# Two-layer graph attention on one core: empty slots of layer 1's gathers get an index past the table's end, and their rows are not read

## The chip, the core and the metric

The kernel runs on one core of a Trainium2 chip. The metric is the device time of one execution in microseconds. Three runs of the kernel before gave 1804.87, 1805.07 and 1805.76 us, so the median is 1805.07 us. One more execution was taken with the hardware profiler, and all durations below come from it.

## The reference

A graph has 3125 nodes with 768 features and 53,125 edges (`src`, `dst`, sorted by `dst`; 25,000 drawn edges in both directions and one self loop for each node). The features are normalised and passed through relu, then two graph attention layers follow, each with a layer norm and a dense residual. The result is added to `x`.

```python
def gat_conv(x, src, dst, W, a_src, a_dst, bias, heads, out_ch, concat):
    xl = (x @ W).reshape(n, heads, out_ch)                 # layer 1: 4 x 256, layer 2: 1 x 768
    alpha_src = jnp.einsum('nhc,hc->nh', xl, a_src)
    alpha_dst = jnp.einsum('nhc,hc->nh', xl, a_dst)
    e = jax.nn.leaky_relu(alpha_src[src] + alpha_dst[dst], 0.2)
    e = jnp.exp(e - jax.ops.segment_max(e, dst, n)[dst])
    alpha = e / (jax.ops.segment_sum(e, dst, n)[dst] + 1e-16)
    return jax.ops.segment_sum(xl[src] * alpha[:, :, None], dst, n) + bias
...
h = relu(layernorm(x))
h1 = relu(layer_norm(gat_conv(h, layer 1))) + (h @ Wr1 + br1)
h2 = layer_norm(gat_conv(h1, layer 2)) + (h1 @ Wr2 + br2)
return x + h2
```

What matters here is the last line of `gat_conv`: for each node, the rows `xl[src]` of its edges are weighted and added.

## The kernel before

**Slots.** The nodes are cut into 25 blocks of 128 (the last has 53). Each block has 17 tiles of 128 slots (the last block has 8), and each slot holds one edge of the block. The four quarters of a block, 32 nodes each, start at slot 0, 512, 1024 and 1536, or where the quarter before has ended if that is later. A node's last self loop takes no slot: its row is added from a plain load (`own`). So the 416 tiles have 53,248 slots, and 50,000 edges fill them. For every slot `rel_s` holds the edge's destination within its block, or -1 where the slot is empty, and `idx_s` holds its source node, or 0 where the slot is empty (L393, L398).

**Stages.** Up to about 300 us the kernel computes `table1` (the rows `xl` of layer 1, 4 KB each, in HBM), packs the slots and looks up the attention terms of destinations. From there to about 500 us it finds the terms of the sources (L1049 to L1060, with the one-hot `ohh` made from `hi_s`, the high part of the source's number) and the softmax weights `al` (`weights`, L576). Then `sums` (L633) does layer 1's sums, and from about 1210 us the second layer runs with a loop of its own.

**Layer 1's sums.** For each tile `fetch` (L685) lets GpSimd issue one indirect DMA (L692), which reads 128 rows of `table1` by the tile's column of `idx_s` into a buffer `g` of 512 KB. There are 13 buffers, taken in turn. `weights_of` (L706) lets VectorE make the tile's matrix `w`: a one-hot of `rel_s` (`oh`, L712) times the softmax weights (L713). An empty slot has `rel_s` = -1, which no column equals, so its weights are 0. TensorE multiplies `w` with `g` into PSUM (`pa`, L732), 256 columns at a time and four quarters beside each other. The tiles of a block come in five rounds (`ROUNDS`): 0, 5, 9, 13; 1, 6, 10, 14; 4, 11, 15; 2, 8, 16; 3, 7, 12. The tiles of the next round are fetched right after a round's matmuls are written down.

**What sets the order.** TensorE, ScalarE and VectorE run in the order in which the program is written. `step` (L644) mixes other work between the rounds: the end of the block before (`end1`, L1123: norm, transposes, and the product with W2, `p` in L182, whose rows go to `table2`), and the residual product of a few late blocks (`more`, `pr` in L182). GpSimd issues the gathers in order. A gather waits until TensorE has read the buffer that it will fill (the gather 13 before), and until the gather 8 before it has landed, since there are eight semaphores in turn (`DMASW0` to `DMASW7`). Once per block GpSimd also gathers the softmax totals (`ao`, L678). The first 13 gathers need no buffer to come free and are issued as soon as `table1` is stored. SyncE's queue carries the plain loads and stores beside the gathers.

The buffers lie in memory that other tiles used before. After the first 13 gathers each buffer holds rows of `table1` in all 128 partitions.

Of the kernel before, what the change touches and what calls it, by code (L numbers as in the profile page):

```python
# [10 lines left out]
F32 = mybir.dt.float32  # L11
# [3 lines left out]
I32 = mybir.dt.int32  # L15
I16 = mybir.dt.int16
AF = mybir.ActivationFunctionType
OP = mybir.AluOpType
# [12 lines left out]
J = 17  # L31
# [4 lines left out]
CODE = 4096  # L36
# [6 lines left out]
@with_exitstack  # L43
def preln_gat2_kernel(
    ctx: ExitStack,
    tc: tile.TileContext,
    x, src, dst,
    W1, a_src1, a_dst1, b1, g1, be1, Wr1, br1,
    W2, a_src2, a_dst2, b2, g2, be2, Wr2, br2,
    out,  # L50
):

    pool = ctx.enter_context(tc.tile_pool(name="flag", bufs=1))
    flag = pool.tile([1, 1], I32, name="flag")
    in_order(tc, x, src, dst, W1, a_src1, a_dst1, b1, g1, be1, Wr1, br1,  # L60
             W2, a_src2, a_dst2, b2, g2, be2, Wr2, br2, out, flag)
    other = tc.nc.values_load(flag[0:1, 0:1], min_val=0, max_val=1)
    with tc.If(other > 0):
        any_order(tc, x, src, dst, W1, a_src1, a_dst1, b1, g1, be1, Wr1, br1,
                  W2, a_src2, a_dst2, b2, g2, be2, Wr2, br2, out)
# [3 lines left out]
def in_order(  # L69
# [16 lines left out]
    nc = tc.nc  # L86
    N, D = x.shape
# [5 lines left out]
    NB = -(-N // P)  # L93
# [28 lines left out]
    def tiles_of(b):  # L122
        return J if b < NB - 1 else JL
# [34 lines left out]
    rel_s = const.tile([128, NB * J], F32, name="rel_s")  # L158
    idx_s = const.tile([128, NB * J], I32, name="idx_s")
    hi_s = const.tile([128, NB * J], F32, name="hi_s")  # L160
    has = const.tile([128, 3, NB], F32, name="has")
    at_last = const.tile([128, NB], I32, name="at_last")
    quarter_i = const.tile([128, 1], I32, name="quarter_i")
# [25 lines left out]
    def load_rows(q, t, src_, b):  # L189

        for o, e in pieces(b):
            q.dma_start(t[o:e], src_[b * P + o:b * P + e, :])
# [440 lines left out]
    def sums(heads, cols, table, al, alo_d, ahead, lag, gp, ap, pp, end, more, pace, first=None, delay=0.0):  # L633
# [4 lines left out]
        width = heads * cols  # L638
        f = width // 2
# [36 lines left out]
        def ask(b):  # L676
            ao = asked[b] = ap.tile([128, 2 * heads, NB], F32, name="ao", bufs=3)
            nc.gpsimd.indirect_dma_start(  # L678
                out=ao.rearrange("p v b -> p (v b)"), out_offset=None, in_=alo_d[:, :],
                in_offset=bass.IndirectOffsetOnAxis(ap=at_last[:, b:b + 1], axis=0))  # L680

        turns = count()
        owns = {}

        def fetch(b, k):  # L685

            got = {}
            for j in ROUNDS[k]:
                if j >= tiles_of(b):
                    continue  # L690
                g = gp.tile([128, width], F32, name=f"g{next(turns) % ahead}", bufs=1)
                nc.gpsimd.indirect_dma_start(  # L692
                    out=g, out_offset=None, in_=table[:, :],
                    in_offset=bass.IndirectOffsetOnAxis(ap=idx_s[:, b * J + j:b * J + j + 1], axis=0))
                got[j] = g, weights_of(b, j)
                place = PLACE[j]
                if place == 4:
                    own = owns[b] = ap.tile([128, width], F32, name="own", bufs=3)
                    load_rows(nc.sync, own, table, b)
                if b == 1 and place == 11:  # L700
                    ask(0)
                if b and place == (13 if tiles_of(b) == J else 5):
                    ask(b)
            return got

        def weights_of(b, j):  # L706

            c = b * J + j
            lo, hi = 32 * QUARTERS[j][0], 32 * QUARTERS[j][-1] + 32
            w = ap.tile([128, heads, hi - lo], F32, name=f"w{hi - lo}", bufs=9 if hi - lo == 32 else 3)  # L710
            oh = ap.tile([128, 68], F32, name="oh", bufs=4)[:, :hi - lo]
            nc.vector.tensor_scalar(oh, iota_f[:, lo:hi], rel_s[:, c:c + 1], None, op0=OP.is_equal)  # L712
            nc.vector.tensor_tensor(w, oh[:, None, :].to_broadcast([128, heads, hi - lo]),  # L713
                                    al[:, POS[j], :, b:b + 1].to_broadcast([128, heads, hi - lo]), OP.mult)
            return w
# [32 lines left out]
    with tc.tile_pool(name="m1", bufs=1) as mp:  # L748
# [8 lines left out]
        with tc.tile_pool(name="h0", bufs=1) as hp, tc.tile_pool(name="pm1", bufs=1, space=PSUM) as pm1, \  # L757
# [238 lines left out]
            with tc.tile_pool(name="pq1", bufs=1, space=PSUM) as pp:  # L996
                with tc.tile_pool(name="sb1", bufs=1) as sb:
# [62 lines left out]
                        next(slots, None)  # L1060
                    for _ in slots:
                        pass
                with tc.tile_pool(name="sr1", bufs=1) as sr:
                    weights(H, own, al1, alo1, keep1, sr, xs1, pp, 4, fill, (5, 13, 8))
                for _ in fill:
# [115 lines left out]
    with tc.tile_pool(name="m2", bufs=1, reuse_waits="tile") as mp, \  # L1181
# [3 lines left out]
        f = C2 // 2  # L1185
# [708 lines left out]
```

## Time and profile before

| | us |
|---|---|
| median of 3 runs | 1805.07 |
| profiled execution | 1801.14 |
| its span, first to last instruction | 1799.2 |
| TensorE busy, whole span | 1637.3 |
| GpSimd busy, whole span | 885.9 |
| first gather of layer 1's sums issued | 307.62 |
| first matmul of layer 1's sums | 503.37 |
| last gather of layer 1 issued | 1153.6 |
| first gather of layer 2 issued | 1211.1 |

The time of an execution is a little more than the span, since it holds what lies before the first and after the last instruction: 1801.14 beside 1799.2 us. In the views, "busy" is the time in which an engine works on instructions, and "idle before" is the time in which it stood still before an instruction, with what ended that wait behind an arrow. PE is TensorE's matmuls, PEld its weight loads, DVE VectorE, ACT ScalarE and POOL GpSimd. `g<-table,idx_s` is a gather; L692 is layer 1's and L1280 layer 2's. The DMA share is the busy share of the 16 DMA engines, and values a little over 1 come from overlapping packets.

### The profile page before, as it was taken

The numbers are of one execution on the slowest core, as the hardware profiler recorded it, in microseconds if no ns is written. First come the engines' busy times: TensorE is split into PE (matmuls) and PEld (weight loads), VectorE is DVE, ScalarE is ACT, GpSimd is POOL, SyncE is SP. The second block draws the span as 40 slices with busy tenths as digits, with TensorE's granted clock in tenths as the row PEclk, the third lists the DMA queues.
The fourth block names the chain that finished last, engine by engine and source line by source line (L and its number), as shares of the span: only waits on it lengthen the run. The fifth ranks groups of instructions, "written<-read, shape, count | busy, mean of one in ns | idle before, by whom it ended". The sixth has DMA issues, their size and how long they took to land. (4 is left out here: it accounts for less than half of the span.)

```text
span 1799.2 us, 43360 instructions
## 1 busy us (share of the span) xinstructions
PE 1637.3 (91%) x17747; PEld 870.2 (48%) x17747; DVE 998.1 (55%) x2639; ACT 454.1 (25%) x1286; POOL 885.9 (49%) x922
## 2 busy tenths in 40 slices
PE   8999999899968999999999999996988888888885
PEld 5666665566534555556554555532333333333331
DVE  7683443788865466566566565632444444444445
ACT  2222332000121222122122112122333333333342
POOL 2000111100055566666566666506777777777772
PEclk9999999999988999999999999998999999999997
DMA  7834546633199999999999999939999999999994
GB/s 239 275 104 136 147 114 192 233 131 123 36 341 407 381 407 407 409 405 410 406 400 411 411 398 400 401 104 387 367 387 380 376 386 386 372 386 384 378 345 148
DMA packets 173719, 562.56 MB, mean 313 GB/s; under 512 B 28610, under 2 KB 53976, under 8 KB 173384
## 3 DMA queue, kind: packets, MB, share of 16 engines
q0 software_dynamic: 100912, 402.06, 58.1%
q1 hardware_dynamic: 68206, 147.26, 23.0%
q10 hardware_dynamic: 4394, 10.39, 1.5%
q8 instruction: 142, 2.33, 0.5%
q14 instruction: 65, 0.53, 0.1%
HBM read 498.62 MB, written 65.62 MB: 314 GB/s over the span
## 5 line engine op out<-in xcount | busy, mean ns | idle before, releaser
L692 POOL DMA_INDIRECT g<-table,idx_s x416 | 407.6, 980 | 404.1 <-DVE m L613 174.7
L1280 POOL DMA_INDIRECT g<-table,idx_s x416 | 421.5, 1013 | 179.2 <-issue 63.7
L732 PE MATMUL pa<-g,w 128*32 128x256 f32 x3912 | 276.5, 389 | 32.0 <-DMA g<-table,idx_s 21.1
L182 PE MATMUL pr<-wr,h 128*32 128x384 f32 (+1 forms) x3136 | 292.4, 504 | 0.0
L182 PE MATMUL p<-w,h1T 128*32 128x384 f32 (+1 forms) x3136 | 283.9, 489 | 2.6 <-DVE h1T L1152 2.6
L732 PEld LDWEIGHTS pa<-g,w 128*32 128x32 f32 x3912 | 144.6, 112 | 146.1 <-issue 28.7
L1347 PE MATMUL pa<-g,w 128*32 128x384 f32 x1956 | 196.3, 509 | 3.1 <-DVE v L1372 3.1
L182 PEld LDWEIGHTS p<-w,h1T 128*32 128x32 f32 x3136 | 123.1, 110 | 125.6 <-issue 85.8
L713 DVE TENSOR_TENSOR w<-oh,al 128x128 f32<-128x128 f32 (+1 forms) x416 | 132.0, 317 | 80.4 <-PE pa L732 45.5
L182 PEld LDWEIGHTS pr<-wr,h 128*32 128x32 f32 (+1 forms) x3136 | 100.6, 112 | 151.0 <-issue 150.1
L1314 DVE CUSTOM_DVE_ANT_0 e<-mix,pen 128x640 f32<-128x640 f32 x25 | 20.6, 824 | 245.5 <-PE mix L1311 245.5
L182 PE MATMUL pr<-h0k,wr 128*32 128x256 f32 (+1 forms) x2304 | 146.9, 391 | 0.9 <-DMA h0k<-h0T_d 0.9
L837 PE MATMUL pm<-w,h0l 128*128 128x344 f32 (+1 forms) x468 | 140.8, 455 | 0.0
L1293 ACT ACTIVATE slots<-g 128x32 f32<-128x32 f32 x416 | 75.1, 222 | 231.4 <-DMA g<-table,idx_s 229.5
L974 PE MATMUL pm<-h0g,wr 128*128 128x512 f32 x288 | 131.7, 604 | 0.0
L837 PE MATMUL pm<-w,h0g 128*128 128x344 f32 x432 | 130.8, 459 | 0.3 <-ACT h0g L816 0.3
L905 POOL DMA_DIRECT2D hot_d<-ohd x25 | 13.4, 537 | 220.1 <-DVE own L491 121.0
L1347 PEld LDWEIGHTS pa<-g,w 128*32 128x32 f32 x1956 | 67.9, 116 | 110.5 <-issue 97.7
L712 DVE TENSOR_SCALAR oh<-iota_f,rel_s 128x32 f32<-128x32 f32 (+1 forms) x416 | 110.9, 267 | 0.1
L182 PEld LDWEIGHTS pr<-h0k,wr 128*32 128x32 f32 x2304 | 80.5, 111 | 55.0 <-issue 9.2
L837 PEld LDWEIGHTS pm<-w,h0l 128*128 128x128 f32 (+1 forms) x468 | 84.8, 185 | 44.1 <-issue 5.7
L1311 PE MATMUL mix<-ident,slots 128*128 128x128 f32 x125 | 22.5, 319 | 88.1 <-ACT slots L1293 88.1
(282 smaller groups left out, 1704.5 us busy)
## 6 DMA issues: line engine op xcount, KB each, us to landing
s<-slo_d SPq DMA_DIRECT2D x25, 544.0 KB
g<-table,idx_s POOLq DMA_INDIRECT x832
table<-row SPq DMA_DIRECT2D x24, 512.0 KB
own<-table SPq DMA_DIRECT2D x24, 512.0 KB
h1T_d<-h1T SPq DMA_DIRECT2D x24, 512.0 KB
h<-h1T_d SPq DMA_DIRECT2D x22, 512.0 KB
table<-row SPq DMA_DIRECT2D x24, 392.0 KB
ring<-in_x_dram SPq DMA_DIRECT2D x24, 384.0 KB
```

The costliest lines, as they stand in the source:

```text
L182: nc.tensor.matmul(out_[o:e], lhsT[:, o:e], rhs, start=start, stop=stop, skip_group_check=True)
L692: nc.gpsimd.indirect_dma_start(out=g, out_offset=None, in_=table[:, :], in_offset=bass.IndirectOffsetOnAxis(ap=idx_s[:, b * J + j:b * J + ...
L712: nc.vector.tensor_scalar(oh, iota_f[:, lo:hi], rel_s[:, c:c + 1], None, op0=OP.is_equal)
L713: nc.vector.tensor_tensor(w, oh[:, None, :].to_broadcast([128, heads, hi - lo]), al[:, POS[j], :, b:b + 1].to_broadcast([128, heads, hi - ...
L732: nc.tensor.matmul(pa[32 * q:32 * q + 32, o // f, o % f:o % f + n], w[:, o // cols, :], g[:, o:o + n], start=to not in opened, stop=False, ...
L837: nc.tensor.matmul(pm[:r, :C], h0[b][:, k, :], w1[:, k, i * C:(i + 1) * C], start=(k == 0), stop=(k == NK1 - 1))
L974: nc.tensor.matmul(pm, wr1[:, k, m * 128:(m + 1) * 128], groups[gi][:, k, :], start=(k == 0), stop=(k == NK1 - 1))
L1280: nc.gpsimd.indirect_dma_start(out=g, out_offset=None, in_=table2[:, :], in_offset=bass.IndirectOffsetOnAxis(ap=idx_s[:, b * J + j:b * J + ...
L1293: nc.scalar.activation(slots[b % 2][:, POS[j], :], gs[b, j][:, C2:C2 + 1].to_broadcast([128, 32]), AF.Copy)
L1311: nc.tensor.transpose(mix[:, c * 128:(c + 1) * 128], at[:, o:o + 4].rearrange("p q n -> p (q n)"), ident)
L1314: nc.vector.tensor_tensor_reduce(out=e, in0=mix[:, :WIN], in1=pen, scale=1.0, scalar=-BIG, op0=OP.add, op1=OP.max, accum_out=top)
L1347: nc.tensor.matmul(pa[32 * q:32 * q + 32, i, :f], w_, g[:, i * f:(i + 1) * f], start=(i, q) not in opened, stop=False, skip_group_check=True)
```

## The change

A second list of indices, `idx_k`, takes the memory of `hi_s`, whose last reader has then run. It equals `idx_s` where a slot holds an edge, and `idx_s + 4096` where it holds none. VectorE makes it in two instructions at the end of the stage of the sources' terms. In layer 1's sums the first 13 gathers go by `idx_s` as before; each later one goes by `idx_k` and carries a bound, `N - 1` = 3124, with `oob_is_err=False`: an index past the bound is no error, and its row is not read. The slot's partition of `g` then keeps what an earlier gather put there, and its weight is 0. In the built program a register move, which writes 3124, stands ahead of each of these gathers on GpSimd. Layer 2 goes by `idx_s` as before.

```diff
     hi_s = const.tile([128, NB * J], F32, name="hi_s")
+    idx_k = hi_s.bitcast(I32)
...
-                g = gp.tile([128, width], F32, name=f"g{next(turns) % ahead}", bufs=1)
-                nc.gpsimd.indirect_dma_start(
-                    out=g, out_offset=None, in_=table[:, :],
-                    in_offset=bass.IndirectOffsetOnAxis(ap=idx_s[:, b * J + j:b * J + j + 1], axis=0))
+                turn = next(turns)
+                g = gp.tile([128, width], F32, name=f"g{turn % ahead}", bufs=1)
+                c = slice(b * J + j, b * J + j + 1)
+                if turn < ahead:
+                    nc.gpsimd.indirect_dma_start(
+                        out=g, out_offset=None, in_=table[:, :],
+                        in_offset=bass.IndirectOffsetOnAxis(ap=idx_s[:, c], axis=0))
+                else:
+                    nc.gpsimd.indirect_dma_start(
+                        out=g, out_offset=None, in_=table[:, :],
+                        in_offset=bass.IndirectOffsetOnAxis(ap=idx_k[:, c], axis=0),
+                        bounds_check=N - 1, oob_is_err=False)
...
                     for _ in slots:
                         pass
+                    none = sb.tile([128, NB * J], F32, name="none")
+                    nc.vector.tensor_scalar(none, rel_s, 0.0, float(CODE), op0=OP.is_lt, op1=OP.mult)
+                    nc.vector.tensor_tensor(idx_k, none, idx_s, OP.add)
```

On VectorE two instructions come in. The rows below are VectorE's order before, at the last two blocks of the sources' terms (`ohh` is the one-hot of a source's high part, `scr<-pq,ohh` the products that pick the term out, `al` the terms themselves).

```order
L545 TENSOR_REDUCE al_116<-scr 128x68 [waits DVE_49]
L1056 TENSOR_TENSOR ohh<-iota_f,hi_s 128x425
L542 TENSOR_TENSOR scr<-pq,ohh 128x500 [waits DVE_49,PE_49]
L542 TENSOR_TENSOR scr<-pq,ohh 128x500 [waits PE_49] x2
L542 TENSOR_TENSOR scr<-pq,ohh 128x200 [waits PE_49]
```

The same place on VectorE with the change:

```order
L546 TENSOR_REDUCE al_116<-scr 128x68 [waits DVE_49]
L1065 TENSOR_TENSOR ohh<-iota_f,hi_s 128x425
L1074 TENSOR_TENSOR hi_s<-none,idx_s 128x425 [waits DVE_49]
L543 TENSOR_TENSOR scr<-pq,ohh 128x500 [waits PE_49] x3
L543 TENSOR_TENSOR scr<-pq,ohh 128x200 [waits PE_49]
```

The add that writes `idx_k` (named `hi_s` here, whose memory it takes) stands between the last `ohh` and the products that use it. The other new instruction, `none<-rel_s`, stands some 170 instructions earlier on VectorE, at the start of the stage. On TensorE, ScalarE and SyncE nothing moves.

On GpSimd the gathers keep their places and their waits. Before, around the fourteenth gather of layer 1:

```order
L692 DMA g_4503<-table_64,idx_s 128x1024 [waits DMASW0_49,DVE_49]
L692 DMA g_4509<-table_64,idx_s 128x1024 [waits DMASW1_49]
L692 DMA g_4515<-table_64,idx_s 128x1024 [waits DMASW2_49,PE_49]
L692 DMA g_4551<-table_64,idx_s 128x1024 [waits DMASW3_49,PE_49]
L692 DMA g_4557<-table_64,idx_s 128x1024 [waits DMASW4_49,PE_49]
```

With the change:

```order
L696 DMA g_4506<-table_64,idx_s 128x1024 [waits DMASW0_49,DVE_49]
L696 DMA g_4512<-table_64,idx_s 128x1024 [waits DMASW1_49]
L700 DMA g_4518<-table_64,hi_s 128x1024 [waits DMASW2_49,PE_49]
L700 DMA g_4556<-table_64,hi_s 128x1024 [waits DMASW3_49,PE_49]
L700 DMA g_4564<-table_64,hi_s 128x1024 [waits DMASW4_49,PE_49]
```

From the fourteenth on the list of indices is the new one; each gather waits for the same lane of semaphores and the same engine as before.

## The prediction

> **What bounds the kernel now.** I read the page's slices first: they say where each engine and the DMA engines are full.
>
> ```profile
> span 1799.2 us, 43360 instructions
> ...
> PE   8999999899968999999999999996988888888885
> ...
> DMA  7834546633199999999999999939999999999994
> GB/s 239 275 104 136 147 114 192 233 131 123 36 341 407 381 407 407 409 405 410 406 400 411 411 398 400 401 104 387 367 387 380 376 386 386 372 386 384 378 345 148
> ```
>
> A slice is 45 us. From the 12th to the 26th, about 500 to 1170 us, stands layer 1's sums. The DMA engines move some 405 GB/s there and TensorE is full too, so either could be the one that sets the pace. The table of windows tells them apart, for the starting stretch, the steady part in two pieces, and the tail:
>
> ```profile
> core 0: us, PE busy (x) PEld busy (x) DVE busy (x) ACT busy (x) POOL busy (x), PEclk, DMA share, GB/s
> 520.00:580.00 60.00, 45.72 (x585) 25.01 (x581) 28.30 (x100) 7.70 (x20) 35.62 (x38) 0.80 1.03 408
> 580.00:800.00 220.00, 219.09 (x3440) 119.19 (x3436) 128.41 (x433) 46.35 (x134) 139.09 (x145) 1.00 1.02 401
> 800.00:1165.00 365.00, 351.28 (x5090) 196.09 (x5085) 225.00 (x747) 71.87 (x204) 236.62 (x249) 1.00 1.02 405
> 1165.00:1215.00 50.00, 46.88 (x466) 19.40 (x460) 17.84 (x56) 10.48 (x26) 3.53 (x5) 0.97 0.38 132
> ```
>
> TensorE stands still for 60 - 45.72 = 14.3 us in the start, 220 - 219.09 = 0.9 us up to 800, 365 - 351.28 = 13.7 us up to 1165, and 3.1 us in the tail: 32.0 us in all. So faster transfers can give no more than 32.0 us, although the DMA engines are full for 650. What ends those waits is in the list of TensorE's waits, asked for 520 to 580 and then for 800 to 1165:
>
> ```profile
> PE pa L732 <- DMA g<-table,idx_s: 12.0, 9, 3.8
> PE pa L732 <- DVE z L670: 2.3, 1, 2.3
> ...
> PE pa L732 <- DMA g<-table,idx_s: 9.2, 12, 1.5
> PE pa L732 <- DVE oh L712: 3.1, 3, 1.9
> PE pa L732 <- DVE aw L666: 1.2, 1, 1.2
> ```
>
> Gathers end 12.0 of the first 14.3 us and 9.2 of the later 13.7. The rest is ended by VectorE, which itself waits for TensorE to free the buffers of `w`, as the groups of 520 to 1215 show:
>
> ```profile
> L713 DVE TENSOR_TENSOR w<-oh,al 128x128 f32<-128x128 f32 x330 | 97.2, 295 | 76.6 <-PE pa L732 45.5 <-DVE oh L712 1.4
> ```
>
> Between 580 and 800 no gather is waited for at all: there TensorE alone sets the pace.
>
> **What is removed.** The slots count 416 x 128 = 53,248, the edges in them 50,000, so 3248 rows are not read. Placing the edges of the inputs by the rules of the windows gives where: none in the first 13 gathers, in 54 of the other 403, mostly in tile 16, a block's fourteenth gather. Block 0 has 123 empty slots, block 1 has 135 (116 in tile 16, 19 in tile 3), block 2 has 74, blocks 3 to 8 have 868, 9 and 10 have 216, and 11 to 24 have 1832. A row is 4096 B, so at 405 GB/s it costs 10.1 ns of all 16 engines, and 3248 rows cost 32.8 us. How much of this is on the path is decided stretch by stretch.
>
> *Start, 520 to 580.* TensorE waits here for one gather after the other, so DMA time is path time. The last wait rows of it:
>
> ```profile
> 553.34 3.89 PE L732 MATMUL pa<-g,w 128*32 128x256 f32 x28 [1.41 <-DMA g<-table,idx_s]
> 558.46 1.03 PE L732 MATMUL pa<-g,w 128*32 128x256 f32 x2 [1.23 <-DMA g<-table,idx_s]
> 560.95 3.20 PE L732 MATMUL pa<-g,w 128*32 128x256 f32 x26 [1.46 <-DMA g<-table,idx_s]
> ```
>
> Counted in the program's order, the matmuls of 561 us are those of block 2's first rounds; its tile 16 comes in the fourth, after the waits. So 123 + 135 = 258 rows count: 258 x 10.1 ns = 2.6 us.
>
> Which of the 16 engines has a row could change this. The Trainium skill, "DMA: Bandwidth & Descriptors", section The descriptor swizzle, says that one engine serves partitions 0 to 3 and 32 to 35, and so on for the others. No view here shows a packet's engine. The empty slots are the last ones of tile 16 (5 to 127 in block 0, 12 to 127 in block 1), so by that rule this engine would be spared 4 + 4 of its rows, not 16; a gather has landed when its last engine is done, and the term would be 1.3 us in place of 2.6.
>
> *580 to 800.* No time on the path. The 868 rows of blocks 3 to 8 and the 216 of 9 and 10 make the DMA engines 10.9 us earlier; what shows is a longer lead of the gathers before TensorE, as far as 13 buffers hold it.
>
> *800 to 1165.* The idle time comes in stretches:
>
> ```profile
> 800.00:850.00 50.00, 49.70 (x768) 31.17 (x763) 32.44 (x109) 10.55 (x30) 33.47 (x36) 1.00 1.03 410
> 850.00:900.00 50.00, 46.40 (x656) 25.53 (x644) 29.20 (x98) 6.72 (x18) 30.06 (x31) 0.97 1.03 406
> 900.00:950.00 50.00, 50.00 (x777) 26.20 (x780) 30.91 (x104) 10.57 (x31) 33.04 (x35) 1.00 1.01 401
> 950.00:1000.00 50.00, 46.57 (x675) 25.55 (x671) 32.39 (x110) 9.02 (x25) 31.98 (x34) 1.00 1.03 411
> 1000.00:1050.00 50.00, 45.57 (x612) 27.42 (x607) 32.51 (x109) 9.19 (x25) 32.16 (x34) 1.00 1.03 411
> 1050.00:1100.00 50.00, 50.00 (x749) 26.42 (x745) 25.87 (x86) 11.75 (x36) 33.14 (x36) 1.00 1.01 399
> 1100.00:1150.00 50.00, 48.03 (x703) 24.71 (x699) 35.09 (x115) 9.90 (x28) 34.75 (x36) 1.00 1.02 394
> ```
>
> The DMA time removed is 1832 x 10.1 ns = 18.5 us in 365, or 2.5 us in each 50. The longest stretch, 950 to 1050, idles 3.4 + 4.4 = 7.9 us; 5.1 us are removed within it and 2.5 in the 50 ahead of it, so it is covered to within 0.3. The others are covered with room. So I take it that the waits for gathers go, 9.2 us, and of the 4.5 us behind VectorE about half, since VectorE's buffers come free earlier when TensorE waits less: 11.4 us, between 9.2 and 13.7. What is late next is TensorE itself.
>
> *The tail.* Layer 2's first gather waits for the last row of `table2`, and the chain that ended last shows it:
>
> ```profile
> 1196.78 10.32 PE p L182 x43
> ...
> 1207.98 0.32 SPq L196
> ...
> 1211.09 7.56 DMA g<-table,idx_s
> ```
>
> TensorE's last products lead to the store and the store to layer 2, so what TensorE gains passes on to layer 2 undiminished. Layer 2 itself keeps its gathers.
>
> **What is added.** *VectorE:* two instructions on 128x425. The nearest rows are the one-hot of the same size and the products behind it, at the end of the sources' stage:
>
> ```profile
> 457.44 0.59 DVE L1056 TENSOR_TENSOR ohh<-iota_f,hi_s 128x425 bf16<-128x425 f32 x1
> 458.48 2.29 DVE L542 TENSOR_TENSOR scr<-pq,ohh 128x500 f32<-128x500 f32 x4 [0.45 <-PE pq L540]
> ...
> 465.12 2.29 DVE L542 TENSOR_TENSOR scr<-pq,ohh 128x500 f32<-128x500 f32 x4 [2.39 <-PE pq L540]
> ```
>
> The add, some 0.6 us, stands just behind that `ohh`. The wait of 0.45 us hides most of it and the next wait for TensorE, 2.39 us, the rest. The compare stands at the start of the stage and is as long; every wait in between takes it up. I count nothing; without that cover it would be 1.2 us. The fourteenth gather now also needs `idx_k`, which is 50 us old by then.
>
> *GpSimd:* nothing in the trace shows a gather with a bound. Its price decides the sign, so here are the rows around it: layer 1's gathers from 520 to 1215, the total's gathers, two gathers issued back to back, and a plain DMA issue of GpSimd.
>
> ```profile
> L692 POOL DMA_INDIRECT g<-table,idx_s x397 | 381.9, 962 | 215.2 <-issue 86.7 <-DMA g<-table,idx_s 58.1 <-PE pa L732 52.9
> L678 POOL DMA_INDIRECT ao<-alo_d,at_last x25 | 25.0, 998 | 13.3 <-DMA g<-table,idx_s 4.8 <-DVE oh L712 4.5 <-issue 3.2
> ...
> 316.17 0.94 POOL L692 DMA_INDIRECT g<-table,idx_s  x1 [0.30 <-issue]
> 317.42 0.94 POOL L692 DMA_INDIRECT g<-table,idx_s  x1 [0.30 <-issue]
> ...
> L905 POOL DMA_DIRECT2D hot_d<-ohd x25 | 13.4, 537 | 220.1 <-DVE own L491 121.0 <-DVE ohd L508 73.0 <-DVE own_r L492 22.9
> ```
>
> A gather takes 0.94 us and 0.30 us pass to the next even with nothing to wait for. Of the idle 215.2 + 13.3 us, 422 x 0.30 = 126.6 are this, so 102 us are true waiting: 102 / 397 = 0.26 us a gather is free. Below that, a dearer gather hides behind buffers and landings. The price of the bound lies between below nothing (fewer rows to write descriptors for, in 54 gathers; these issues are off the path anyway) and, as an upper row, what handling 128 indices costs now: 0.94 - 0.54 = 0.40 us. I take under 0.1 us, the register move and a compare, since the indices are already walked one by one; that is hidden.
>
> **Sum.** Against the profiled 1801.1 us: -2.6 - 11.4 = -14.0, so 1787.1. Against the median, 3.9 us higher: 1805.1 - 14.0 = 1791.1 us. A difference under 0.2%, 3.6 us, can hardly be told from none.
>
> **The rivals.**
>
> *GpSimd becomes the bound, slower.* At 0.40 us more, 397 x 0.40 = 159 us meet 102 free: +57 us, 1862, and the saving in rows is worth nothing, since the transfers then wait for their issue. It decides from 0.26 us a gather. For it speaks how little room there is; against it that the instruction and its list of 128 indices are the same. The Trainium skill, "GPSIMD Engine Reference", section 3.1, speaks for it: branching that depends on data costs about 12 cycles an element; at its 1.2 GHz an estimate from that page is 128 x 10 ns = 1.28 us a gather on one core, and the kernel would take some 2200 us. No row shows such a branch. Chance 0.24.
>
> *TensorE is the bound anyway.* If the waits after 800 only change their releaser from gathers to VectorE's `oh` and `w`, the start's 2.6 us is all: 1802.5, within 0.2%. For it: 4.5 us already end at VectorE. Against it: VectorE is busy for 225 of 365 us. Chance 0.08.
>
> *The rows are not spared.* If an index past the bound still takes a transfer of its slot, everything stays: 1805.1. The trace has no such gather. Chance 0.08.
>
> **How the numbers follow.** The forecast has 0.60. Its low end: the weight loads wait for gathers as well, and if that time lay wholly beside the matmuls' waits, it would add to the gain.
>
> ```profile
> PEld pa L732 <- DMA g<-table,idx_s: 10.6, 9, 1.9
> ```
>
> That is 2.6 + 13.7 + 10.6 = 26.9 us, 1778; I take 1779. The high end must take in both cases without gain (1802.5, 1805.1) and the mild part of the first rival, 0.02 us a gather past the threshold: 397 x 0.02 = 8 us, 1813. Beyond it lies most of the first rival, some 0.2. Faster by over 0.2%: 0.60; within: 0.16; slower: 0.24.
>
> **What would show it.** Right: back-to-back gathers of layer 1 still some 1.24 us apart; the software queue's bytes lower by 3248 x 4096 B = 13.3 MB; TensorE's waits for `g` after 800 near 0 and idle time from 800 to 1165 under 5 us; in the start 2 to 3 us less; layer 2's first gather 14 us earlier and layer 2 as long as before. The forecast is wrong if gathers of layer 1 are 1.5 us or more apart with nothing to wait for (first rival), if TensorE idles as long with VectorE as releaser (second), or if the bytes stay (third).

## The result, and the profile after

The changed kernel takes 1790.45 us, the median of 6 runs (1787.15 to 1801.98), against 1804.62 us for 6 runs of the kernel before beside it (1797.27 to 1805.76). The ratio is 0.9933, with a 95% interval of 0.9909 to 0.9956: 12 us less, 8 to 16 with the interval. The two medians lie 14.2 us apart and the two profiled spans 11.4. The profiled execution took 1789.67 us, its span 1787.8. The forecast was 1791.1, which is 14.0 us less than the 1805.1 it set out from.

First, were rows spared? The row of the software queue says so, here of the kernel before and then, with the page's slices, of the one after:

```profile
q0 software_dynamic: 100912, 402.06, 58.1%
```

```profile
DMA  7833545633179999999999999929999999999994
GB/s 239 270 103 131 150 122 170 258 124 129 42 288 406 362 384 401 391 402 391 407 398 396 410 380 363 391 87 393 362 382 382 380 387 386 377 384 383 371 348 159
...
q0 software_dynamic: 100912, 388.76, 57.3%
```

13.30 MB are gone, which is 3248 rows of 4096 B. The number of packets is unchanged at 100,912: in place of each spared row a small packet is left, and the page's count of packets under 512 B rises by 3248, from 28,610 to 31,858. The slices still show full DMA engines through layer 1's sums, at a slightly lower rate.

Where the time went can be seen if the span is cut at the same work in both kernels: from the first matmul of layer 1's sums (`pa`) in four pieces to the first gather of layer 2. The windows before:

```profile
core 0: us, PE busy (x) PEld busy (x) DVE busy (x) ACT busy (x) POOL busy (x), PEclk, DMA share, GB/s
503.40:595.80 92.40, 74.70 (x969) 43.73 (x973) 44.85 (x145) 14.22 (x34) 54.68 (x53) 0.83 1.02 404
595.80:802.10 206.30, 205.39 (x3206) 109.83 (x3202) 125.35 (x424) 44.47 (x128) 132.09 (x138) 1.00 1.02 401
802.10:1174.30 372.20, 358.48 (x5164) 199.19 (x5158) 230.70 (x763) 72.16 (x205) 235.67 (x248) 1.00 1.02 404
1174.30:1211.10 36.80, 33.68 (x313) 13.34 (x309) 10.13 (x31) 8.62 (x24) 0.01 (x1) 0.95 0.17 54
```

And after:

```profile
505.20:595.40 90.20, 74.13 (x968) 43.46 (x972) 45.73 (x145) 14.23 (x34) 57.21 (x53) 0.87 1.02 400
595.40:801.10 205.70, 205.42 (x3207) 108.84 (x3202) 127.00 (x424) 44.47 (x128) 139.92 (x139) 1.00 1.00 386
801.10:1165.50 364.40, 354.06 (x5164) 193.48 (x5158) 230.66 (x763) 72.17 (x205) 246.41 (x246) 1.00 1.00 389
1165.50:1200.60 35.10, 31.98 (x313) 12.72 (x309) 10.13 (x31) 8.53 (x23) 0.01 (x1) 1.00 0.17 56
```

The matmul counts agree to one, so each pair is the same work:

| stretch | before | after | difference |
|---|---|---|---|
| up to the first matmul | 503.4 | 505.2 | +1.8 |
| start | 92.4 | 90.2 | -2.2 |
| the 3206 matmuls behind it | 206.3 | 205.7 | -0.6 |
| steady part, 5164 matmuls | 372.2 | 364.4 | -7.8 |
| tail, to layer 2's first gather | 36.8 | 35.1 | -1.7 |
| layer 2, to the end | 588.1 | 587.2 | -0.9 |
| span | 1799.2 | 1787.8 | -11.4 |

In the steady part TensorE's idle time fell from 372.20 - 358.48 = 13.7 us to 364.40 - 354.06 = 10.3 us. That is only 3.4 of the 7.8; the other 4.4 us came out of time that the table counts as busy, for the same 5164 matmuls at the same granted clock, 1.00. The tail's 1.7 us are all busy time, at a granted clock of 1.00 in place of 0.95; nothing in the profile ties them to the change. What TensorE still waits for, in the start and then in the steady part:

```profile
PE pa L741 <- DMA g<-table,hi_s: 8.8, 6, 3.8
PE pa L741 <- DVE oh L721: 2.7, 2, 1.6
...
PE pa L741 <- DMA g<-table,hi_s: 6.7, 9, 1.3
PE pa L741 <- DVE oh L721: 2.2, 2, 1.2
PE pa L741 <- DVE w L722: 1.4, 1, 1.4
```

Waits for gathers went from 12.0 to 8.8 us and from 9.2 to 6.7. They did not go away. Where the busy time shrank is found by asking for the groups on TensorE from 802 to 1166 us in both kernels, which is the steady part without 8 of its `pa` matmuls before and 9 after:

```profile
L732 PE MATMUL pa<-g,w 128*32 128x256 f32 x2192 | 153.6, 381 | 13.7 <-DMA g<-table,idx_s 9.2 <-DVE oh L712 3.1 <-DVE aw L666 1.2
```

```profile
L741 PE MATMUL pa<-g,w 128*32 128x256 f32 x2192 | 149.6, 382 | 10.3 <-DMA g<-table,hi_s 6.7 <-DVE oh L721 2.2 <-DVE w L722 1.4
```

As many matmuls with the gathered rows cover 4.0 us less, while the mean of one stays (381 and 382 ns). So the gaps between them closed, gaps that the pipelined matmul ahead covers in the record. A count over exactly the same matmuls of the steady part says the same: from the start of each matmul to the start of the next, without the idle time that the profile shows, `pa` took 136.1 us before and 132.5 after, `pr` 59.7 and 58.6, and the products `p`, which read no gathered row, 163.7 and 163.9. The weight loads' list agrees: their wait for `g` between 800 and 1165 was 10.6 us before and is now

```profile
PEld pa L741 <- DMA g<-table,hi_s: 5.7, 5, 1.7
```

The new cost on GpSimd, in two gathers issued back to back and in the group of 520 to 1215:

```profile
521.52 0.99 POOL L700 DMA_INDIRECT g<-table,hi_s  x1 [0.30 <-issue]
522.82 1.01 POOL L700 DMA_INDIRECT g<-table,hi_s  x1 [0.30 <-issue]
...
L700 POOL DMA_INDIRECT g<-table,hi_s x398 | 403.7, 1014 | 186.9 <-issue 78.5 <-PE pa L741 61.9 <-DMA g<-table,hi_s 29.1
```

A bounded gather takes 0.99 us in place of 0.94, so 1.29 us lie between the starts of two in place of 1.24. The waits for gathers to land (the lane of eight) fell from 58.1 to 29.1 us, those for TensorE to free a buffer rose from 52.9 to 61.9: the transfers are earlier, as the rows spared would have it. Not all of it is the rows', though: in the run with the bound alone, below, the same two waits are 46.6 and 55.9 us, so 11.5 of the 29.0 us come with the dearer issue. On VectorE:

```profile
459.25 0.59 DVE L1065 TENSOR_TENSOR ohh<-iota_f,hi_s 128x425 bf16<-128x425 f32 x1
459.88 0.60 DVE L1074 TENSOR_TENSOR hi_s<-none,idx_s 128x425 int32<-128x425 f32 x1
...
466.94 2.30 DVE L543 TENSOR_TENSOR scr<-pq,ohh 128x500 f32<-128x500 f32 x4 [2.39 <-PE pq L541]
```

The add stands where the order put it and takes 0.60 us; the wait of 0.45 us behind it is gone, and the next one still is 2.39 us.

### The profile page after: what moved, and what is told of

Its sections match the earlier page's. It is cut to its first block, busy times and chain, and to the rows that moved or that the text cites. A ratio compares the mean times of both kernels' runs of the same rounds, so it can differ in the third digit from the quotient of the medians.

```text
span 1787.8 us, 43764 instructions
## 1 busy us (share of the span) xinstructions
PE 1631.8 (91%) x17747; PEld 862.8 (48%) x17747; DVE 1001.2 (56%) x2641; ACT 453.4 (25%) x1286; POOL 907.5 (51%) x922
## 3 DMA queue, kind: packets, MB, share of 16 engines
q0 software_dynamic: 100912, 388.76, 57.3%
## 5 line engine op out<-in xcount | busy, mean ns | idle before, releaser
L1292 POOL DMA_INDIRECT g<-table,idx_s x416 | 421.7, 1014 | 180.5 <-issue 67.3
L700 POOL DMA_INDIRECT g<-table,hi_s x403 | 412.9, 1025 | 194.5 <-issue 79.1
L183 PE MATMUL pr<-wr,h 128*32 128x384 f32 (+1 forms) x3136 | 296.1, 510 | 0.0
L741 PE MATMUL pa<-g,w 128*32 128x256 f32 x3912 | 269.5, 389 | 27.0 <-DMA g<-table,hi_s 15.5
L1359 PE MATMUL pa<-g,w 128*32 128x384 f32 x1956 | 192.6, 502 | 3.2 <-DVE v L1384 3.2
L183 PEld LDWEIGHTS p<-w,h1T 128*32 128x32 f32 x3136 | 117.0, 110 | 129.8 <-issue 95.3
L696 POOL DMA_INDIRECT g<-table,idx_s x13 | 15.1, 1158 | 181.8 <-DVE m L614 175.8
```

The source lines that it names most:

```text
L183: nc.tensor.matmul(out_[o:e], lhsT[:, o:e], rhs, start=start, stop=stop, skip_group_check=True)
L700: nc.gpsimd.indirect_dma_start(out=g, out_offset=None, in_=table[:, :], in_offset=bass.IndirectOffsetOnAxis(ap=idx_k[:, c], axis=0), bound ...
L741: nc.tensor.matmul(pa[32 * q:32 * q + 32, o // f, o % f:o % f + n], w[:, o // cols, :], g[:, o:o + n], start=to not in opened, stop=False, ...
L1292: nc.gpsimd.indirect_dma_start(out=g, out_offset=None, in_=table2[:, :], in_offset=bass.IndirectOffsetOnAxis(ap=idx_s[:, b * J + j:b * J + ...
L1359: nc.tensor.matmul(pa[32 * q:32 * q + 32, i, :f], w_, g[:, i * f:(i + 1) * f], start=(i, q) not in opened, stop=False, skip_group_check=True)
```

## The experiments

**Theory.** Layer 1's sums are paced by TensorE together with nearly full DMA engines; rows that are not moved shorten TensorE's waits, open and hidden, and the bound's 0.05 us a gather lies in GpSimd's free time. Rivals: the gain comes from the bound itself or from the new list (B), it comes from no longer reading one row 0 thousands of times (C), and the price on GpSimd eats a larger gain or would decide at a slightly higher price (the prediction's first rival). The measure used beside the ratio is layer 1's length, from its first to its last `pa` matmul, which the windows count as 9347 to 9349 matmuls in every kernel. Before and after:

```profile
503.37:1176.20 672.83, 640.50 (x9348) 353.86 (x9352) 400.93 (x1331) 130.88 (x367) 422.44 (x438) 0.97 1.02 402
```

```profile
505.20:1167.40 662.20, 635.52 (x9349) 346.87 (x9353) 403.40 (x1331) 130.87 (x367) 443.54 (x438) 0.98 1.00 389
```

That is 672.8 us with 32.3 idle, and 662.2 with 26.7. One profile gives this length to about 2 us: the three kernels that read all rows took 672.8, 673.5 and 672.0 us, and the three with the change's layer 1 (two of them alter layer 2 besides) 662.2, 663.4 and 659.8. All ratios below are to the kernel before, run beside each.

**The bound without the saving.** The second list equals the first; every bounded gather stays bounded.

```diff
-                    nc.vector.tensor_scalar(none, rel_s, 0.0, float(CODE), op0=OP.is_lt, op1=OP.mult)
+                    nc.vector.tensor_scalar(none, rel_s, 0.0, 0.0, op0=OP.is_lt, op1=OP.mult)
```

> The bound and the register moves stay, but the added 4096 is 0, so no index is past the bound and every row is read. Theory A (the gain is DMA time of rows that are not read): no gain, 1804.6 us within 3, the software queue's bytes back at 402 MB, gathers still 0.99 us long on GpSimd (the bound's price, 0.05 us, hidden in the 0.26 us that are free). If the bound's 0.05 us were on the path, 397 x 0.05 = 20 us slower.

Measured: 1806.23 us, ratio 1.0002 (0.9987 to 1.0016); a gather takes 0.99 us; layer 1 is

```profile
508.40:1181.90 673.50, 640.78 (x9349) 362.08 (x9353) 402.15 (x1331) 130.85 (x367) 442.96 (x438) 0.98 1.02 402
```

The bound makes GpSimd 20 us busier (422 to 443) and layer 1 no longer. The gain is in the rows, B falls.

**Other rows in place of row 0.** No bound; an empty slot reads the row of its partition's number.

```diff
-                        in_offset=bass.IndirectOffsetOnAxis(ap=idx_k[:, c], axis=0),
-                        bounds_check=N - 1, oob_is_err=False)
+                        in_offset=bass.IndirectOffsetOnAxis(ap=idx_k[:, c], axis=0))
...
-                    nc.vector.tensor_scalar(none, rel_s, 0.0, float(CODE), op0=OP.is_lt, op1=OP.mult)
+                    nc.vector.tensor_scalar(none, rel_s, 0.0, node_f, op0=OP.is_lt, op1=OP.mult)
```

> No bound and no skipping: an empty slot reads row p (its partition, 0 to 127) in place of row 0, so the same bytes move. Theory A and theory B (the least spared DMA engine sets the gain): as before, 1804.6 us within 3. Theory C (what was dear is some 100 reads of the one row 0 in a gather): most of the gain, about 1791 us.

Measured: 1802.05 us, ratio 0.9983 (0.9969 to 0.9997), layer 1 672.0 us. Spreading the reads gives at most 0.3% and most likely 0.2%, a quarter of the gain; layer 1 does not show it beyond the 2 us. C falls as the main cause.

**The same bytes from a few partitions.** 3224 rows are left out on partitions 0 to 3 and 32 to 35, edges or not.

```diff
-                    nc.vector.tensor_scalar(none, rel_s, 0.0, float(CODE), op0=OP.is_lt, op1=OP.mult)
-                    nc.vector.tensor_tensor(idx_k, none, idx_s, OP.add)
+                    nc.vector.tensor_scalar(rows_i, node_i, 92, None, op0=OP.bitwise_and)
+                    nc.vector.tensor_scalar(rows_f, rows_i, 0.0, float(CODE), op0=OP.is_equal, op1=OP.mult)
+                    nc.vector.tensor_scalar(idx_k, idx_s, rows_f, None, op0=OP.add)
```

> Instead of the empty slots, partitions 0 to 3 and 32 to 35 of each gather from the fourteenth on are left out (edges among them: 8 rows a gather, 3224 rows, as many as the change spares). Theory A, with rows dealt to the 16 engines in any even way: about as the change, 1790 us. Theory B, with the skill's rule that one DMA engine serves just these partitions: the other 15 have all their rows, no gain, 1804 us within 3, though the bytes fall by 13.2 MB.

**The same bytes from partitions spread out.** Again 3224 rows, from partitions 0, 4 .. 28 in every other gather and 64, 68 .. 92 in the ones between.

```diff
+                    nc.vector.tensor_scalar(rows_i, node_i, 99, None, op0=OP.bitwise_and)
+                    for i in range(2):
+                        nc.vector.tensor_scalar(rows_f[:, i:i + 1], rows_i, 64.0 * i, float(CODE),
+                                                op0=OP.is_equal, op1=OP.mult)
+                        nc.vector.tensor_scalar(idx_k[:, i::2], idx_s[:, i::2], rows_f[:, i:i + 1], None, op0=OP.add)
```

> Again 8 rows a gather are left out (3224 rows, edges among them), but of partitions 0, 4, ... 28 in even columns and 64, 68, ... 92 in odd ones, which by the skill's rule are one row of each engine in two gathers. Theory A: as the change, 1790 us. Theory B: every engine is spared 6.25%, twice what the change spares the engine with the fewest (104 of 3248 rows, a mean of 203): 1786 to 1789 us, faster than the change.

Measured: few partitions 1802.51 us, ratio 0.9984 (0.9971 to 0.9996), layer 1 669.7 us; spread out 1792.06 us, ratio 0.9929 (0.9911 to 0.9946), layer 1 656.8 us. The queue's row, layer 1's window and TensorE's wait for gathers from 800 to 1165, first of the few partitions, then spread out:

```profile
q0 software_dynamic: 100912, 388.86, 56.1%
...
504.30:1174.00 669.70, 638.55 (x9349) 348.20 (x9353) 406.84 (x1331) 130.62 (x367) 442.72 (x438) 0.98 0.97 384
...
PE pa L741 <- DMA g<-table,hi_s: 8.6, 12, 1.3
```

```profile
q0 software_dynamic: 100912, 388.86, 57.1%
...
507.00:1163.80 656.80, 632.11 (x9349) 348.92 (x9353) 404.86 (x1331) 130.87 (x367) 443.09 (x438) 0.98 1.01 392
...
PE pa L741 <- DMA g<-table,hi_s: 2.0, 3, 0.7
```

Both move the same bytes with the same instructions, and the first gains 3.1 us in layer 1, the second 16.0. The DMA share fits this reading: 0.97 against 1.01, and 1.02 before; one engine of 16 without rows should take about 0.06 off, while the others are as full as ever. So a row goes with an engine by its partition, and what counts most is the engine that is spared least. That rows are tied to engines by these partitions is what the Trainium skill, "DMA: Bandwidth & Descriptors", section The descriptor swizzle, states for a plain transfer to 128 partitions; the partitions of the two kernels were chosen by its rule, and the runs agree with it, for gathers.

The steady part alone, by the same matmuls in each trace, took 373.2 us before, 365.4 after the change, 370.1 with few partitions and 360.0 spread out. The change's empty slots lie uneven, over the partitions (104 rows for the least spared engine where the mean is 203, as the expectation counts them) and over time (mostly in one gather of a block), and layer 1 gains 10.6 us from about as many rows as the spread-out kernel turns into 16.0. Which of the two costs more is open: no run leaves out rows that are even over the engines and bunched in time. (The two medians differ less than the intervals: other stages, 2.5 us between the layers among them, were longer in that profile.)

**Half of all rows.** Every odd partition is left out of the bounded gathers, to find the ceiling.

```diff
+                    nc.vector.tensor_scalar(rows_i, node_i, 1, None, op0=OP.bitwise_and)
+                    nc.vector.tensor_scalar(rows_f, rows_i, float(CODE), None, op0=OP.mult)
+                    nc.vector.tensor_scalar(idx_k, idx_s, rows_f, None, op0=OP.add)
```

> From the fourteenth gather on the odd partitions are left out (half of all rows, edges among them, 106 MB less, the same for each DMA engine). This gives the ceiling of what fewer rows can give. Theory A: TensorE waits for no gather after 560 us, and the time falls by the 12.0 + 9.2 us of waits for gathers and the 4.4 us that hid in the busy time: about 1778 us. If waits for gathers stay (issue, latency or the 13 buffers end them, not DMA time): 1786 to 1790 us, with a list of waits as after the change.

Measured: 1762.12 us, ratio 0.9756 (0.9735 to 0.9778), more than expected.

```profile
505.00:1138.00 633.00, 622.32 (x9347) 326.95 (x9349) 406.45 (x1332) 131.16 (x367) 444.05 (x438) 0.99 0.82 261
...
PE pa L741 <- DMA g<-table,hi_s: 6.2, 6, 1.4
```

Layer 1 is 39.8 us shorter than before: 32.3 - 10.7 = 21.6 us idle and 640.5 - 622.3 = 18.2 us "busy". Of the busy time 5.8 us lie in the start, at a granted clock of 0.93 in place of 0.83. In the steady part, at 1.00 in both, 11.9 us of busy and 13.1 us of idle time are gone; 10.9 of the busy time are in `pa` (136.1 to 125.2 us), and none in `p` (163.7 and 163.6). So with the DMA engines full, nearly as much of the wait for gathers hides inside busy as shows as idle, and the 32.0 us of the prediction were no ceiling.

**Fewer buffers.** 11 in place of 13 for `g`, the change otherwise.

```diff
-            sums(H, C1, table1, al1, alo1_d, 13, 3, gp, ap, pp, end1, more, (2.5, 3.8, 0, 0, 0.9), first(), -6.3)
+            sums(H, C1, table1, al1, alo1_d, 11, 3, gp, ap, pp, end1, more, (2.5, 3.8, 0, 0, 0.9), first(), -6.3)
```

> The change with 11 buffers of g in place of 13. If the waits for gathers that are left after the change (6.7 us after 800) come from rounds with little other work, which use gathers faster than they land and empty the lead that the buffers hold, 2 x 1.28 us less of lead costs up to 2.6 us in each of five such places: 5 to 12 us slower than the change, about 1799 us. If they come from DMA time over longer stretches: as the change, 1790.5 us within 3.

Measured: 1799.67 us, ratio 0.9966 (0.9949 to 0.9983), layer 1 669.1 us, 6.9 longer than with 13. Two buffers are worth two thirds of the change's gain, so in the changed kernel the lead that the buffers hold is worth time of the same order as the rows. The kernel before was not run with 11 buffers; whether spared rows work by this lead is argued, not shown.

**The change in layer 2 as well.** From the 37th gather of layer 2 on, by the second list with the bound.

```diff
+                    nc.gpsimd.indirect_dma_start(
+                        out=g, out_offset=None, in_=table2[:, :],
+                        in_offset=bass.IndirectOffsetOnAxis(ap=idx_k[:, c], axis=0),
+                        bounds_check=N - 1, oob_is_err=False)
```

> The change, and the same in layer 2 from its 37th gather on (RING is 36), with the same list of indices. Theory A: some 2990 rows of 3136 B, 9.4 MB, are spared at 386 GB/s: 24 us of DMA time, in a layer where the chain of work that ended last is mostly gathers: 10 to 20 us faster than the change, 1770 to 1780 us. Theory B: less than half of that, since the empty slots lie in the upper partitions: 1783 us.

Measured: 1809.05 us, ratio 1.003 (1.0014 to 1.0045). All that the change gained is lost again: layer 2, from its first `pa` matmul, takes 557.0 us, and 539.5 in the change. Its gathers, and 400 us of it, in the change and then with both layers:

```profile
L1292 POOL DMA_INDIRECT g<-table,idx_s x416 | 421.7, 1014 | 180.5 <-issue 67.3 <-DMA hot<-hot_d 46.2 <-ACT slots L1305 23.7
...
1300.00:1700.00 400.00, 348.81 (x3904) 140.97 (x3908) 184.23 (x378) 151.63 (x459) 304.91 (x301) 0.95 1.01 381
```

```profile
L1298 POOL DMA_INDIRECT g<-table,hi_s x380 | 408.1, 1074 | 117.8 <-issue 60.1 <-ACT slots L1312 26.3 <-DMA g<-table,hi_s 16.2
...
1300.00:1700.00 400.00, 336.41 (x3726) 136.27 (x3722) 174.30 (x358) 149.18 (x442) 310.17 (x291) 0.94 0.97 351
```

GpSimd is busy for 304.91 us with 301 instructions, and 301 x 0.30 = 90 us pass between them: 395 of 400 us. Nothing is free, although the DMA share is 1.01. The price of the bound, 380 x 0.05 = 19 us, is paid almost in full: 17.5 us in this profile, and the two ratios, 1.003 and 0.9933, are 17.5 us apart as well. The transfer rate falls from 381 to 351 GB/s, about half of it because rows are not read (the next run falls to 367 at nearly the old price of an issue) and half with the slower issue. The bytes of the software queue fell by a further 9.36 MB (to 379.40) for nothing. This is the prediction's first rival, in the layer that the change left alone.

**Only the gathers with many empty slots.** Layer 2's tile 16 alone carries the bound, 22 gathers with 2334 of its empty slots.

```diff
-                if asked < RING:
+                if asked < RING or j != 16:
```

> Layer 1 as in the change. In layer 2 only the gathers of tile 16 from the 37th gather on (22 of 380, which hold 2334 of its empty slots) go by the second list with the bound; the other 358 go as before. Theory (layer 2 is bound by GpSimd's issue, so only the price of the bound matters there, and rows are worth nothing): 22 x 0.05 = 1 us more than the change, 1789 to 1793 us. Rival (layer 2 is bound by its transfers as well, and the bound's price hid a gain in the run with both layers): 2334 rows of some 3 KB at 390 GB/s are 18 us, of which at least a third shows: 1785 us or less.

**The same in layer 1.** There too only tile 16, 24 gathers.

```diff
-                if turn < ahead:
+                if turn < ahead or j != 16:
```

> As the kernel before it in this call, and in layer 1 too only tile 16 carries the bound: 24 gathers instead of 403, with 2573 of the 2990 empty slots. Theory (in layer 1 the bound's 0.05 us is covered and the rows pay): the gain shrinks with the rows, by 417 of 2990, so 1 to 2 us less gain than the change: 1790 to 1794 us. Rival (the bound's price is paid in layer 1 as well, and the change's gain is what is left of a larger one): 379 x 0.05 = 19 us come back in part, 1785 us or less.

Measured: 1792.58 us, ratio 0.9931 (0.9905 to 0.9957), and 1795.73 us, ratio 0.9934 (0.991 to 0.9958). Neither can be told from the change. The window of layer 2 with its tile 16 bounded:

```profile
1300.00:1700.00 400.00, 345.96 (x3895) 139.97 (x3891) 183.23 (x376) 154.03 (x462) 305.53 (x302) 0.95 0.99 367
```

14 GB/s less and as many GpSimd instructions, and layer 2 takes 539.6 us beside 539.5 in the change: in layer 2 spared rows are worth nothing that shows. In layer 1 the bound on 24 gathers does what the bound on 403 does, so its price was no loss there that can be seen. (That expectation sets 2573 rows against 2990, which is layer 2's number; layer 1's is 3248, and 675 rows fewer at 10.1 ns are at most 7 us of transfers, of which the profile's 663.0 us of layer 1 show 0.8.) No version that still computes everything beat the change beyond the noise.

**A dearer issue, the first time.** An iota on GpSimd behind each bounded gather, left to the scheduler.

```diff
+                    nc.gpsimd.iota(spare, pattern=[[1, 128]], base=0, channel_multiplier=0)
```

> The change, and behind each gather from the fourteenth on a GpSimd iota of 128x128 (0.23 us, some 0.25 with its dispatch), which nobody reads. It tests the threshold of the prediction's first rival, 0.26 us a gather. With the bound's 0.05 us it is 0.30 us dearer than before: 397 x 0.30 = 119 us against 102 free, so GpSimd sets the pace: +17 us on before, about 1820 us. If GpSimd has more room than the sum says: 1790 us, as the change.

Measured: 1797.32 us, ratio 0.9959 (0.9942 to 0.9975), but all 403 iotas ran in the first 200 us, ahead of all of layer 1's gathers, and the bounded gathers are 1.29 us apart as in the change. Layer 1 took 663.2 us, 1.0 more than in the change. The loss lies ahead of it: the iotas start at 18.8 us and hold up GpSimd's transfer `views_d<-pk_d` from 48.9 to 57.3 us, and with it the first matmul of layer 1's sums from 505.2 to 512.4. A miss: it says nothing of the threshold.

**A dearer issue, in place.** GpSimd too follows the program's order in layer 1's sums, once with an iota of 128 elements a partition, once with 256.

```diff
-        with tc.manual_schedule(engines={PE, ACT, DVE}):
+        with tc.manual_schedule(engines={PE, ACT, DVE, POOL}):
...
+                    nc.gpsimd.iota(spare, pattern=[[1, 128]], base=0, channel_multiplier=0)
```

> The change, with an iota of 128x128 on GpSimd right behind each of the 403 bounded gathers, in place (GpSimd too follows the program's order in layer 1's sums). An iota of this size takes 0.23 us in the trace of the change; with the change 186.9 + 10.2 - 423 x 0.30 = 70 us of layer 1's gathers are free, 0.18 us a gather. Theory of a threshold: only what lies past it is paid, 0.05 x 403 = 20 us at most, so 1795 to 1812 us. If every added time passes on in full (the waits for buffers lie behind the issue, so that nothing hides): 403 x 0.23 = 93 us, some 1880 us. If issue has no part in the pace: 1790 us.

> As the kernel before it in this call with an iota of 128x256. Rows of 128x1 (0.12 us) and 128x128 (0.23 us) give 0.34 us for it, an estimate. Theory of a threshold: (0.34 - 0.18) x 403 = 64 us over the change, 1840 to 1860 us, so each further 0.1 us a gather costs 40 us once the 0.18 are used up. If every added time passes on in full: 137 us, some 1927 us. If issue has no part in the pace: 1790 us.

Measured: 1799.55 us, ratio 0.9966 (0.995 to 0.9981), and 1824.78 us, ratio 1.0101 (1.0078 to 1.0125). Rows of GpSimd, layer 1's window and TensorE's wait for gathers, with 128 and then with 256:

```profile
527.63 1.00 POOL L701 DMA_INDIRECT g<-table,hi_s  x1 [0.17 <-issue]
528.63 0.26 POOL L705 IOTA spare<- 128x128 int32 x1
529.05 0.99 POOL L701 DMA_INDIRECT g<-table,hi_s  x1 [0.17 <-issue]
...
506.50:1176.30 669.80, 638.53 (x9349) 357.56 (x9353) 410.24 (x1331) 130.63 (x367) 554.80 (x841) 0.99 1.00 384
...
PE pa L743 <- DMA g<-table,hi_s: 22.4, 24, 3.2
```

```profile
522.24 1.00 POOL L701 DMA_INDIRECT g<-table,hi_s  x1 [0.16 <-issue]
523.26 0.36 POOL L705 IOTA spare<- 128x256 int32 x1
523.78 1.00 POOL L701 DMA_INDIRECT g<-table,hi_s  x1 [0.17 <-issue]
...
506.60:1199.80 693.20, 651.12 (x9349) 375.42 (x9353) 458.62 (x1331) 130.95 (x367) 590.05 (x841) 0.98 0.99 371
...
PE pa L743 <- DMA g<-table,hi_s: 32.0, 36, 3.7
```

An iota of 0.26 us moves the next gather by only 0.13 us, from 1.29 to 1.42 us between starts: the idle gap ahead of a gather is 0.17 us in these rows, in place of 0.30. The longer one moves it to 1.54. So the added time is less than both expectations counted, and the second lies 15 us below its range. Layer 1 then takes 662.2, 669.8 and 693.2 us: 7.6 us for the first 0.13, 23.4 for the next 0.12. In full, these would be 403 x 0.13 = 52 and 403 x 0.12 = 48 us. So there is a threshold, but a soft one, as would follow if the free time is not the same at every gather. The sign turns between 1.42 and 1.54 us; a straight line between the two ratios crosses 1 at 1.45, an estimate, 0.21 us above the 1.24 of before, where the prediction had 0.26. No run has GpSimd in the program's order without an iota, so a part of the order itself is not excluded. One thing disturbs the larger run: VectorE's busy time rises from 403 to 459 us. It is the one-hots, here after the change and then with 256, both from 510 to 1160 us:

```profile
L722 DVE TENSOR_TENSOR w<-oh,al 128x128 f32<-128x128 f32 x334 | 98.3, 294 | 66.9 <-PE pa L741 35.8 <-PE pr L183 0.5
L721 DVE TENSOR_SCALAR oh<-iota_f,rel_s 128x32 f32<-128x32 f32 x333 | 89.4, 268 | 0.2
```

```profile
L723 DVE TENSOR_SCALAR oh<-iota_f,rel_s 128x32 f32<-128x32 f32 x324 | 124.2, 383 | 0.2
L724 DVE TENSOR_TENSOR w<-oh,al 128x128 f32<-128x128 f32 x324 | 96.1, 297 | 55.1 <-PE pa L743 24.4 <-PE pr L184 0.5
```

VectorE still stands idle for 55.1 us ahead of `w`, so it is not busy throughout, and the open waits that grew most are those for gathers (15.5 us in layer 1 after the change, 32.0 here). How much of the 23.4 us is VectorE's part was not separated.

## Why the prediction was right, and where not

**The sum, 14.0 us, lies within what was measured (8 to 16 us by the ratio, 11.4 in the profile); its largest term was put together wrongly.** The step that failed: "So I take it that the waits for gathers go, 9.2 us, and of the 4.5 us behind VectorE about half", 11.4 us from 800 to 1165, for "the DMA time removed is 1832 x 10.1 ns". The runs put in its place:

- The waits for gathers fell by 2.5 us, idle time by 3.4. The 10.1 ns a row hold only if all engines share the saving. With 8 rows left out of each of 223 gathers, 1784 rows spread evenly, the waits for gathers of this stretch did fall to 2.0 us and the steady part by 13.2; with the same number on one engine's partitions they stayed at 8.6, and the steady part fell by 3.1. The change's rows lie between the two: 6.7 and 7.8. A second assumption is doubtful: the longest stretch was to draw on time saved in the stretches ahead of it, but two buffers fewer cost 6.9 us, so the lead is near its limit; no run tests this by itself. After the change 950 to 1000 still idles 3.6 us and 1000 to 1050 2.7, where the prediction had them covered to within 0.3:

```profile
950.00:1000.00 50.00, 46.36 (x642) 25.22 (x634) 34.59 (x113) 10.49 (x29) 35.46 (x36) 0.97 1.02 402
1000.00:1050.00 50.00, 47.31 (x659) 30.12 (x662) 31.85 (x108) 6.55 (x19) 34.53 (x34) 1.00 1.03 408
```

- 4.4 us came out of busy time, 3.6 of them in the `pa` matmuls, as the weight loads' wait for gathers fell from 10.6 to 5.7. The prediction had this only as its low end. "Faster transfers can give no more than 32.0 us" was wrong: leaving out half of the rows gave 39.8.

Together the steady part gave 7.8 us where the term was 11.4. The rest of the profiled gain, which happens to be 11.4 us too, is 2.2 us in the start, 1.7 in the tail at a higher clock, 0.9 in layer 2 and 0.6 between 595 and 801, less 1.8 that the first matmul came later. All of these but the start's are of the size in which single executions differ, and no run ties them to the change. So the mechanism was right, the size of its largest term was too large by 3.6 us, and the total agrees partly by chance.

**Start:** 2.2 us for a term of 2.6 (1.3 with rows tied to engines by partition); 1.6 of it idle, the wait for gathers 3.2 lower, another taking its place in part. It lies between the two and does not decide between them; the pair of runs does. One thing said ahead of the prediction bears on this stretch: of the 13 gathers issued "as soon as `table1` is stored" the trace before shows 11, from 307.6 to 321.1 us; the 12th and the 13th wait for VectorE until 496.8 and 499.6, just ahead of the first matmul at 503.4.

**580 to 800:** 0.6 us for 0, right.

**VectorE:** 0.60 us hidden, right, by the very rows named.

**GpSimd:** 0.05 us for "under 0.1", hidden in layer 1, shown by the bound alone (1.0002) and by the bound on 24 gathers (0.9934). The Trainium skill's rule on branching, "GPSIMD Engine Reference", section 3.1, gave an estimate of 1.28 us a gather; the gather's 0.05 us do not agree with it. The first rival's mechanism exists, with its threshold at about 0.21 (the estimate above) in place of 0.26; the small price, which no row of before showed, kept it away.

**Layer 2:** its first gather came 10.5 us earlier, where 14 was said, and from there it is as long as before within 1 us. With the bound there as well, the first rival holds in it, as the run with both layers shows.

**The other rivals:** the bytes fell, so the rows are spared; that TensorE is the bound anyway holds for 595 to 801 alone, where it idles for 0.3 us.

## What to carry to other kernels

Before work is saved on an indirect gather, add its engine's busy time and the fixed gap of every issue: where they fill the stretch, as 395 of 400 us in layer 2, 0.05 us a gather costs more than the saved 9.4 MB are worth, and the edit pays only where that sum leaves room. Count saved rows by DMA engine, so by partition: the same number of rows was worth 3.1 us on one engine and 16.0 on all. And do not take an engine's idle time as the ceiling of what faster transfers can give; the weight loads' waits, and the busy time of the matmuls that read the transfers, hold more of it.

## What the hardware showed unasked

- Where a gather's index is past the bound, its bytes are not moved, but the queue's count of packets stays: 100,912 with 402.06, 388.76 and 296.51 MB. A packet under 512 B is left for each such row.
- Rows of a gather are tied to DMA engines by their partition (layer 1 3.1 against 16.0 us shorter for the same 3224 rows).
- An iota behind a gather takes 0.26 us and costs 0.13: the gap between two gathers is partly free for another kind of instruction.
- An iota of 256 elements a partition beside VectorE's one-hots made them 383 ns in place of 268, while the products `w` stayed at 297 and 294.
